# Later 32x32 transposes, longer DMA pieces and later products in the self-attention of the second block

## The chip, the cores and the metric

The kernel runs on one core of a Trainium2 chip. The metric is the device time of one execution in microseconds. TensorE multiplies matrices into PSUM, VectorE (DVE) and ScalarE (ACT) read PSUM and SBUF, GpSimd (POOL) and SyncE (SP) issue most of the DMAs. Each engine runs its own instructions in a fixed order and waits on semaphores for the others.

## The reference

Four attention blocks run in sequence on `x` of 4 batches x 1024 tokens x 256 channels (float32). Their context is 4 x 77 x 256. Block L1 is the one that matters here. It has three layers; the first attends to the context, and the second and third attend to themselves, with 4 heads of 64 channels over 1024 tokens:

```python
Q = relu(q @ Wq + bq); K = relu(k @ Wk + bk); V = relu(v @ Wv + bv)   # 4 heads of 64
scores = einsum('hbqd,hbkd->hbqk', Qh, Kh) / sqrt(64)
scores = where(key_mask == 0, NEG, scores)
attn = softmax(scores, axis=-1) * query_mask
out = einsum('hbqk,hbkd->hbqd', attn, Vh)
out = layer_norm(out + q, gamma, beta)
enc = leaky_relu(out @ Wff + bff, 0.2) + out
```

For the product with V the softmax numerators, which come out with queries on the partitions, must be turned so that keys are on the partitions.

## The kernel before

Work is cut into items: one layer for one batch. The two self layers of L1 are eight items of class `Self4`, and each has 16 units. A unit (`scores(p, t)`) is one pair of heads `p` (two of the four) and one tile `t` of 128 queries against all 1024 keys. Two consecutive units, `t` even and `t` odd, share one tile `PR` and one tile `PT`, and are called a pair below.

What happens to a unit, in order:

1. TensorE forms the scores of both heads (L1262) in two PSUM tiles `ss` of two banks each. The pool `pb` has just these two, so the next unit's scores wait until this unit's exponentials have read them.
2. VectorE takes each head's maximum (L1273, tile `nm`). ScalarE takes the exponential (L1279) and writes it to `PR`, sorted so that blocks of 32 keys which go to the same 32 partitions stand together (index `c`).
3. VectorE turns all 32x32 blocks of the unit in place (`turned_by_blocks`, L1291).
4. After the odd unit, 16 DMAs (L1298) carry 32 partitions x 4 KB each from `PR` to `PT`, one for each pair of a source group `a` and a target group `c` of 32 partitions. SP issues eight and POOL eight. This completes the turn.
5. TensorE multiplies by V (`weighted`, L1334), half of the keys in one unit and the other half in the next, and one unit later `normal` scales the result and adds it to `x`.

`PR` (tag E) and `PT` (tag B) have two buffers each. The exponential of the first unit of a pair can therefore start only when all 16 DMAs of the pair before last have landed.

TensorE's order is written by hand: `Pipe.unit` issues, for each unit, what is due as "full", the scores, what is due as "next", a share of other steps (`pump`: projections and transposes of neighbouring items, the feed-forward of the item before), and then what is due as "turn", "late" and "col". `pipe.later(kind, delay, f)` puts a step `delay` units ahead. The orders of VectorE, ScalarE, SP and POOL are made by a scheduler when the program is built. `tc.issue_after(ins)` binds what is issued inside its block behind `ins` in the order of the engine; it adds no wait. The attribute `net.blocks` is true in the branch that runs here.

Of the kernel before, what the change touches and what calls it, by code (L numbers as in the profile page):

```python
# [13 lines left out]
ALU = mybir.AluOpType  # L14
AX = mybir.AxisListType
PSUM = bass.MemoryType.PSUM

P = 128
NB, S, C, SC = 4, 1024, 256, 77
NT = S // P  # L20
# [102 lines left out]
class Pipe:  # L123
# [15 lines left out]
    def unit(self, scores=None, cost=0.0):  # L139
        self.call("full")  # L140
        if scores:
            scores()
        self.call("next")
        self.now += cost
        self.pump()
        for kind in ("turn", "late", "col"):
            self.call(kind)
        self.u += 1

    def run(self, items):  # L150
        pump = Pump(self, 1, items[0].start(), [])
        pump.until(lambda: items[0].halves >= 1)
        left = pump.lists[0]
        before = None
        for a, b in zip(items, items[1:]):
            b.prev = a
        for i, item in enumerate(items):
            last = i + 1 == len(items)
            first = left + ([] if last else items[i + 1].start())
            second = (before.end() if before else []) + (item.end() if last else [])  # L160
            left = []
            idle = item.idle()
            self.pump = pump = Pump(self, item.units + idle, item.more() + first, second)
            for _ in range(idle):
                self.unit()
            for scores in item.attend():
                self.unit(scores, item.cost)
            assert last or not any(pump.lists)
            before = item
        while self.due:  # L170
            pump.n = 0
            self.unit()
        pump.n = pump.units - 1
        pump()
# [33 lines left out]
class Cross16(Item):  # L208
# [147 lines left out]
    def scores(self, g, c):  # L356

        net, h = self.net, H16
        nc = net.nc
        e, s = g // 2, g % 2  # L360
        if g % 2 == 0:
            self.pts = net.tile("B", [SC, 2, h.J, 512], name="PT")
        pt = self.pts[:, g % 2]
        pbs = [net.pb.tile([P, 2, 512], F32, tag="pb", name="pb") for _ in range(2)]
        for j in range(h.J):
            rows = slice(32 * j, 32 * j + 32)
            nc.tensor.matmul(  # L367
                pbs[j // 2][:SC, j % 2, :], self.ka[rows, e, 2 * (j % 2) + s, :], self.qt[rows, e, ts(c, 512)],
                start=True, stop=False,
            )  # L370
        for j in range(h.J):
            rows = slice(32 * j, 32 * j + 3 * G)
            nc.tensor.matmul(  # L373
                pbs[j // 2][:SC, j % 2, :], net.pick16[rows, g, :], self.sh[rows, c, :], start=False, stop=True
            )
        for i in range(2):
            nc.scalar.activation(pt[:, 2 * i : 2 * i + 2, :], pbs[i][:SC], AF.Exp, scale=self.l.scale)  # L377
        net.pipe.later("col", 0, lambda: self.weighted(g, c, pt))

    def weighted(self, g, c, pt):  # L380
        net, l, h = self.net, self.l, H16
        nc = net.nc
        po = net.p1.tile([P, 512], F32, tag="p1", name="po")
        for j in range(h.J):
            col = self.head(g, j) * h.vs
            nc.tensor.matmul(  # L386
                po[ts(j, h.slot), :], l.v[:, self.b, col : col + h.vw], pt[:, j, :], start=True, stop=True
            )
        ot = net.tile("OT", [P, 512], name="OT")
        net.evac(ot, po)  # L390
        net.pipe.later("late", 1, lambda: self.normal(g, c, ot))
# [249 lines left out]
class Layer16Self:  # L641


    scale, norm, eps, out, ff, has_wo = 0.25, 1, None, None, None, True
# [168 lines left out]
class LayerFew:  # L813
# [3 lines left out]
    scale, norm, eps, out, ff, has_wo = 0.25, 1, None, None, None, True  # L817
# [303 lines left out]
class Self4(Item):  # L1121
# [133 lines left out]
    def scores(self, p, t):  # L1255
        net = self.net
        nc = net.nc
        ss = [net.pb.tile([P, 2, 512], F32, tag="pb", name="ss") for _ in range(2)]
        for k in range(2):
            for h in range(2):  # L1260
                rows = slice(64 * h, 64 * h + 64)
                nc.tensor.matmul(  # L1262
                    ss[h][:, k, :], self.qk[p][rows, 0, ts(t, P)], self.qk[p][rows, 1, ts(k, 512)],
                    start=True, stop=True,
                )
        if not net.blocks:
            pr = net.tile("E", [P, 2, S], name="PR")
        elif t % 2 == 0:
            self.pr = net.tile("E", [P, 2, 2, S], name="PR")
        for h in range(2):  # L1270
            at = slice(2 * p + h, 2 * p + h + 1)
            s2 = ss[h].rearrange("p k n -> p (k n)")
            nc.vector.tensor_reduce(self.nm[:, t, at], s2, AX.X, ALU.max, negate=True)  # L1273
            if net.blocks:
                out = self.pr[:, t % 2, h, :].rearrange("p (c k i) -> p k c i", c=4, i=32)
                s2 = s2.rearrange("p (k c i) -> p k c i", c=4, i=32)
            else:
                out = pr[:, h, :]
            nc.scalar.activation(out, s2, AF.Exp, bias=self.nm[:, t, at], accum_out=self.sums[:, t, at])  # L1279
        if net.blocks:  # L1280
            net.pipe.later("next", 1, lambda pr=self.pr: self.turned_by_blocks(p, t, pr))
        else:
            net.pipe.later("full", 1, lambda: self.turned(p, t, pr))

    def turned_by_blocks(self, p, t, pr):


        net = self.net
        nc = net.nc
        part = pr[:, t % 2].rearrange("p h s -> p (h s)")  # L1290
        nc.vector.transpose(part, part)  # L1291
        if t % 2 == 0:
            return

        pt = net.tile("B", [P, 2, 2, 4, NT, 32], name="PT")
        for c in range(4):
            for a in range(4):
                (nc.sync, nc.gpsimd)[a % 2].dma_start(  # L1298
                    out=pt[ts(c, 32), :, :, a].rearrange("p t h k j -> p (t h) (k j)"),
                    in_=pr[ts(a, 32), :, :, ts(c, 256)].rearrange("p t h n -> p (t h) n"),  # L1300
                )
        state = []
        for half in range(2):
            net.pipe.later("turn", 2 + half, lambda half=half: self.weighted(p, t, pt, half, state))

    def turned(self, p, t, pr):

# [16 lines left out]
    def weighted(self, p, t, pts, half, state):  # L1324
        net = self.net
        nc = net.nc
        if half == 0:
            state.append(net.p1.tile([P, 2, P], F32, tag="p1", name="po"))
        po = state[0]
        if net.blocks:  # L1330
            po = po.rearrange("p t (a j) -> p t a j", a=4)
        for k in range(4 * half, 4 * half + 4):
            for h in range(2):
                nc.tensor.matmul(  # L1334
                    po[64 * h : 64 * h + 64], self.v[:, k, 64 * (2 * p + h) : 64 * (2 * p + h) + 64],
                    pts[:, :, h, :, k, :] if net.blocks else pts[:, :, h, k, :], start=k == 0, stop=k == NT - 1,
                )
        if half:
            if t % 4 == 1:
                self.ot = net.tile("OT", [P, 4, P], name="OT")  # L1340
            at = t % 4 - 1
            net.carry(self.ot[:, at : at + 2, :], state[0])
            if at:
                net.pipe.later("late", 1, lambda ot=self.ot: self.normal(p, t - 3, ot))
# [853 lines left out]
```

## Time and profile before

| | |
|---|---|
| median of 3 runs | 2405.5 us (2398.03 to 2406.79) |
| profiled execution, its own time | 2396.79 us |
| its span, first to last instruction | 2394.9 us |
| granted TensorE clock, mean of the span | 0.958 |
| busy share of the span: TensorE, VectorE, ScalarE, POOL | 92%, 66%, 39%, 16% |
| first and last maximum of the self layers (L1273) start | 950.2 us, 1874.0 us |
| a transpose (L1291), mean of 128 | 2311 ns |
| an exponential (L1279), mean of 256 | 1114 ns |
| a maximum (L1273), mean of 256 | 1210 ns |
| issue of a DMA from PR to PT: POOL, SP, median | 552 ns, 806 ns |

The profiled execution is the base of every duration. Busy time is summed over an engine's instructions; matmuls are pipelined and their ends are modelled, so that a matmul that waits in the middle of a group shows as a longer one. "Idle before" is the time an engine stood still ahead of an instruction, put down to what released it.

### The profile page before, as it was taken

Reading aid. Unit: us, or ns where it says so; the run is one execution under the profiler, and the core shown is the slowest. Engines: PE = TensorE matmul, PEld = TensorE weight load, DVE = VectorE, ACT = ScalarE, POOL = GpSimd, SP = SyncE. Lnnn points to the kernel's source line nnn. Section 1 sums busy time; section 2 is a strip of 40 time slices with the busy share of each in tenths; the row PEclk is TensorE's granted clock in tenths of the full one; section 3 lists DMA queues with packets and bytes.
Section 4 is the critical chain, followed back from the end, with each engine's and each line's share of the span. In section 5 each row is a group of like instructions: output and inputs, shape, how many; then the busy total and the mean of one; then the engine's idle time right before and its main releaser. Section 6 shows DMA issues by size and latency. Waiting matters only on the chain. (4 is left out here: it accounts for less than half of the span.)

```text
span 2394.9 us, 31195 instructions
## 1 busy us (share of the span) xinstructions
PE 2204.3 (92%) x11035; PEld 1204.8 (50%) x11035; DVE 1582.6 (66%) x3167; ACT 930.2 (39%) x1828; POOL 380.4 (16%) x648
## 2 busy tenths in 40 slices
PE   6899999999898979999999899999999899999996
PEld 3565446566577655545454445454545344444442
DVE  6665553534424565888888788888888656656765
ACT  2222332222232355545454454444444234434333
POOL 2000000000000000333333233333333100000000
PEclk8999989989998998999999999999999899999988
DMA  5000010000000000667776577766787400000000
GB/s 147 1 3 14 5 36 1 1 3 5 12 1 7 1 5 1 146 147 152 151 156 144 123 151 157 151 142 141 148 163 143 97 5 1 5 1 1 27 18 28
DMA packets 148677, 158.01 MB, mean 66 GB/s; under 512 B 51432, under 2 KB 130849, under 8 KB 148513
## 3 DMA queue, kind: packets, MB, share of 16 engines
q1 hardware_dynamic: 122161, 85.63, 17.2%
q0 software_dynamic: 25296, 69.24, 13.1%
q8 instruction: 91, 1.49, 0.3%
q10 hardware_dynamic: 1056, 1.05, 0.1%
q14 instruction: 73, 0.60, 0.1%
HBM read 17.41 MB, written 4.19 MB: 9 GB/s over the span
## 5 line engine op out<-in xcount | busy, mean ns | idle before, releaser
L1279 ACT ACTIVATE PR<-ss,nm 128x1024 f32<-128x1024 f32 x256 | 284.7, 1114 | 366.2 <-DVE nm L1273 290.2
L1291 DVE STREAM_TRANSPOSE PR<-PR 128x2048 f32<-128x2048 f32 x128 | 295.8, 2311 | 128.9 <-ACT PR L1279 114.3
L1298 POOL DMA_DIRECT2D PT<-PR x512 | 279.6, 554 | 577.7 <-PE ss L1262 236.7
L1262 PE MATMUL ss<-QK 64*128 64x512 f32 x1024 | 324.8, 628 | 28.8 <-ACT PR L1279 28.5
L1273 DVE TENSOR_REDUCE nm<-ss 128x1 f32<-128x1024 f32 x256 | 299.6, 1210 | 13.8 <-PE ss L1262 13.8
L377 ACT ACTIVATE PT<-pb 77x1024 f32<-77x1024 f32 x192 | 185.4, 1015 | 193.2 <-PE pb L373 193.2
L1334 PE MATMUL po<-PT,V 128*64 128x256 f32 x2048 | 251.1, 387 | 5.1 <-DMA PT<-PR 5.1
L281 DVE TENSOR_REDUCE mx<-pa 128x4 f32<-128x308 f32 x384 | 161.4, 470 | 83.7 <-PE pa L276 82.5
L1262 PEld LDWEIGHTS ss<-QK 64*128 64x128 f32 x1024 | 113.3, 187 | 176.8 <-ACT PR L1279 99.7
L1334 PEld LDWEIGHTS po<-PT,V 128*64 128x64 f32 x2048 | 136.6, 137 | 108.4 <-issue 51.1
L276 PE MATMUL pa<-KA,QT 64*128 64x308 f32 x768 | 169.1, 486 | 14.0 <-DVE mx L281 12.8
L1545 POOL TENSOR_TENSOR pw<-va,minus_half 128x4 f32<-128x4 f32 (+1 forms) x28 | 38.8, 1384 | 714.5 <-DVE va L1543 542.0
L386 PE MATMUL po<-PT,Vc 77*32 77x512 f32 x768 | 140.4, 639 | 7.6 <-ACT PT L377 7.0
L276 PEld LDWEIGHTS pa<-KA,QT 64*128 64x128 f32 x768 | 84.3, 193 | 99.1 <-issue 37.0
L604 PE MATMUL pp<-hF,w 128*128 128x256 f32 x512 | 116.9, 382 | 0.0
L367 PE MATMUL pb<-QT,KA 32*77 32x512 f32 x768 | 114.1, 665 | 0.0
L619 PE MATMUL pp<-w,hid 128*128 128x256 f32 x512 | 113.7, 379 | 0.0
L619 PEld LDWEIGHTS pp<-w,hid 128*128 128x128 f32 x512 | 97.0, 190 | 16.5 <-issue 2.2
L604 PEld LDWEIGHTS pp<-hF,w 128*128 128x128 f32 x512 | 95.6, 190 | 18.2 <-issue 6.0
L266 PE MATMUL pp<-hT,wq 128*128 128x512 f32 x192 | 98.0, 646 | 5.5 <-ACT hT L1507 5.0
L1536 DVE BATCH_NORM_STATS2 st<-x 128x6 f32<-128x256 f32 x256 | 97.7, 403 | 3.2 <-DMA x<-in_x 2.3
L1405 PE MATMUL pp<-wo,hE 128*128 128x256 f32 x384 | 96.4, 393 | 1.6 <-ACT hE L1512 1.6
(256 smaller groups left out, 3079.5 us busy)
## 6 DMA issues: line engine op xcount, KB each, us to landing
PT<-PR SPq DMA_DIRECT2D x512, 128.0 KB
PT<-PR POOLq DMA_DIRECT2D x512, 128.0 KB, 4.9
x<-in_x SPq DMA_DIRECT2D x4, 1024.0 KB
out<-x SPq DMA_DIRECT2D x8, 512.0 KB
w<-in_ff_w SPq DMA_DIRECT2D x2, 1024.0 KB
gb<-in_norms POOLq DMA_DIRECT2D x5, 256.0 KB, 6.6
wk<-in_l_wk SPq DMA_DIRECT2D x10, 128.0 KB
wv<-in_l_wv SPq DMA_DIRECT2D x5, 256.0 KB
```

The costliest lines, as they stand in the source:

```text
L276: nc.tensor.matmul(pas[i], self.qt[rows, e, ts(t, P)], self.ka[rows, e, :, :], start=True, stop=True)
L281: nc.vector.tensor_reduce(out, pas[i].rearrange("p (j s) k -> p j s k", s=2), AX.X, ALU.max, negate=True)
L377: nc.scalar.activation(pt[:, 2 * i : 2 * i + 2, :], pbs[i][:SC], AF.Exp, scale=self.l.scale)
L386: nc.tensor.matmul(po[ts(j, h.slot), :], l.v[:, self.b, col : col + h.vw], pt[:, j, :], start=True, stop=True)
L604: nc.tensor.matmul(pp[:, i, :], self.w1[:, cc, ts(f + i, P)], s["hT"][:, cc, ts(q, 2 * P)], start=cc == 0, stop=cc == NC - 1)
L619: nc.tensor.matmul(pp[:, u, :], s["a"][:, f, ts(u, P)], self.w2[:, f, :], start=f == 0, stop=f == NF - 1)
L1262: nc.tensor.matmul(ss[h][:, k, :], self.qk[p][rows, 0, ts(t, P)], self.qk[p][rows, 1, ts(k, 512)], start=True, stop=True,)
L1273: nc.vector.tensor_reduce(self.nm[:, t, at], s2, AX.X, ALU.max, negate=True)
L1279: nc.scalar.activation(out, s2, AF.Exp, bias=self.nm[:, t, at], accum_out=self.sums[:, t, at])
L1291: nc.vector.transpose(part, part)
L1298: (nc.sync, nc.gpsimd)[a % 2].dma_start(out=pt[ts(c, 32), :, :, a].rearrange("p t h k j -> p (t h) (k j)"), in_=pr[ts(a, 32), :, :, ts(c, ...
L1334: nc.tensor.matmul(po[64 * h : 64 * h + 64], self.v[:, k, 64 * (2 * p + h) : 64 * (2 * p + h) + 64], pts[:, :, h, :, k, :] if net.blocks e ...
```

## The change

It does four things in `scores` and `turned_by_blocks`, for the eight self items only. The maxima are remembered, and the transpose of a unit is bound behind the maxima of the unit that follows it. The dimensions of `PR` and `PT` are reordered, so that each of the 16 DMAs reads and writes one run of 4 KB in each partition instead of four of 1 KB. SP issues twelve of them and POOL four (those with `a == 3`). The two halves of the product with V move from the end of the third and fourth unit after the pair to just behind the scores of the fourth and fifth.

```diff
-            self.pr = net.tile("E", [P, 2, 2, S], name="PR")
+            self.pr = net.tile("E", [P, 4, 2, 2, S // 4], name="PR")
...
-            nc.vector.tensor_reduce(self.nm[:, t, at], s2, AX.X, ALU.max, negate=True)
+            net.reduced = nc.vector.tensor_reduce(self.nm[:, t, at], s2, AX.X, ALU.max, negate=True)
             if net.blocks:
-                out = self.pr[:, t % 2, h, :].rearrange("p (c k i) -> p k c i", c=4, i=32)
+                out = self.pr[:, :, t % 2, h, :].rearrange("p c (k i) -> p k c i", i=32)
...
-        part = pr[:, t % 2].rearrange("p h s -> p (h s)")
-        nc.vector.transpose(part, part)
+        part = pr[:, :, t % 2].rearrange("p c h n -> p c (h n)")
+        with net.tc.issue_after(net.reduced.ins):
+            nc.vector.transpose(part, part)
...
-        pt = net.tile("B", [P, 2, 2, 4, NT, 32], name="PT")
+        pt = net.tile("B", [P, 4, 2, 2, NT, 32], name="PT")
         for c in range(4):
             for a in range(4):
-                (nc.sync, nc.gpsimd)[a % 2].dma_start(
-                    out=pt[ts(c, 32), :, :, a].rearrange("p t h k j -> p (t h) (k j)"),
-                    in_=pr[ts(a, 32), :, :, ts(c, 256)].rearrange("p t h n -> p (t h) n"),
+                (nc.gpsimd if a == 3 else nc.sync).dma_start(
+                    out=pt[ts(c, 32), a].rearrange("p t h k j -> p (t h k j)"),
+                    in_=pr[ts(a, 32), c].rearrange("p t h n -> p (t h n)"),
                 )
...
-            net.pipe.later("turn", 2 + half, lambda half=half: self.weighted(p, t, pt, half, state))
+            net.pipe.later("next", 3 + half, lambda half=half: self.weighted(p, t, pt, half, state))
...
-                    pts[:, :, h, :, k, :] if net.blocks else pts[:, :, h, k, :], start=k == 0, stop=k == NT - 1,
+                    pts[:, :, :, h, k, :].rearrange("p a t j -> p t a j") if net.blocks else pts[:, :, h, k, :], start=k == 0, stop=k == NT - 1,
```

## The prediction

> **What bounds the kernel now.** I read the busy times by stage first. The eight self items fill 950 to 1910 us; 1060 to 1780 us is their undisturbed middle. The columns are the stretch, its length, then busy time and count for TensorE, weight loads, VectorE, ScalarE and POOL, the granted clock, the DMA share and GB/s.
>
> ```profile
> 1060.00:1780.00 720.00, 686.52 (x3348) 338.47 (x3344) 599.61 (x778) 342.27 (x701) 231.28 (x412) 0.99 0.70 147
> ```
>
> TensorE looks full. The groups of the same stretch say otherwise (count, then busy time and mean of one, then idle time before them and what ended it):
>
> ```profile
> L1262 PE MATMUL ss<-QK 64*128 64x512 f32 x788 | 247.6, 627 | 18.0 <-ACT PR L1279 17.9
> L1273 DVE TENSOR_REDUCE nm<-ss 128x1 f32<-128x1024 f32 x198 | 231.9, 1211 | 11.9 <-PE ss L1262 11.9
> L1291 DVE STREAM_TRANSPOSE PR<-PR 128x2048 f32<-128x2048 f32 x99 | 228.8, 2311 | 103.2 <-ACT PR L1279 90.3 <-DMA PT<-PR 12.8
> L1279 ACT ACTIVATE PR<-ss,nm 128x1024 f32<-128x1024 f32 x197 | 219.1, 1114 | 295.1 <-DVE nm L1273 233.6 <-issue 40.8 <-DMA PT<-PR 19.2
> L1334 PE MATMUL po<-PT,V 128*64 128x256 f32 x1584 | 192.8, 385 | 0.0
> ```
>
> 198 maxima are 99 units, so a unit lasts 720/99 = 7.27 us. An undelayed group of eight score matmuls takes 1.99 us (next fence), 197 us for 99 units. The 247.6 us shown hold 51 us of waiting inside the groups, and 18 us stand before them. Without these 69 us TensorE needs 651/99 = 6.6 us per unit. ScalarE waits for VectorE (233.6 us), and VectorE hardly waits for scores (11.9 us): it is 83% busy, and stands 103 us ahead of its transposes. So VectorE sets the pace, with maxima 2.36, a wait for the exponentials, transpose 2.31, and the small work between. The timeline of one unit shows that chain:
>
> ```profile
> 1198.58 2.32 DVE L1273 TENSOR_REDUCE nm<-ss 128x1 f32<-128x1024 f32 x2
> 1201.37 1.13 ACT L1279 ACTIVATE PR<-ss,nm 128x1024 f32<-128x1024 f32 x1
> 1202.62 2.31 DVE L1291 STREAM_TRANSPOSE PR<-PR 128x2048 f32<-128x2048 f32 x1 [1.73 <-ACT PR L1279]
> 1204.00 1.99 PE L1262 MATMUL ss<-QK 64*128 64x512 f32 x8
> 1205.00 1.24 SPq L1298 DMA_DIRECT2D PT<-PR  x2
> 1206.02 1.22 DVE L1273 TENSOR_REDUCE nm<-ss 128x1 f32<-128x1024 f32 x1 [0.33 <-PE ss L1262]
> ```
>
> From maxima to the end of the transpose is 6.35 us, with nothing else done. Last, the DMA view of 1195 to 1235 us, one figure per us:
>
> ```profile
> DMA  9999996000068999999990000068999999999007
> GB/s 205 214 268 227 168 199 108 0 0 0 8 136 213 250 224 211 278 228 200 191 160 17 0 16 0 0 133 214 252 228 180 299 234 194 198 207 208 13 0 160
> ```
>
> The transpose ends at 1204.93; 16 DMAs of 128 KB then keep all engines full until 1216.6. The trace's completion updates give 12.4 us from the end of the odd unit's transpose to the last landing (mean of 47 pairs). I call this L.
>
> **The change, part by part.** *The tie.* The transpose of unit u now follows the maxima of u+1 on VectorE (the built order shows maxima, transpose, small work in every unit). Its exponentials are then done, so the wait (90 of the 103 us, 0.9 us per unit) goes. VectorE then needs 599.6/99 = 6.06 us per unit, under TensorE's 6.6. But the small work (6.06 minus 2.36 and 2.31, 1.4 us on average) is uneven. In two of an item's 16 units the layer norm (six to eight passes L1583 and L1586 of 0.47, less overlap) brings it to about 4.2 us, and the unit before each has 2.4. There the maxima come 2.4 + 4.7 - 6.6 = 0.5 and then 0.5 + 4.7 + 4.2 - 6.6 = 2.8 us late. Scores wait only if maxima are over 1.25 us late: the second exponential ends 3.75 us after the maxima begin (3.92 here, 1198.58 to 1202.50, with a copy of ScalarE's between), the three quarters of the next group that need its PSUM tile take 1.6 more (of 1.99), and 6.6 - 5.35 = 1.25. So 1.55 us are lost twice in 16 units, 0.19 per unit: 6.79 us per unit if nothing else binds.
>
> What is late next is the buffer `PR`. Landing used to count from the transpose right behind the exponential; now it counts from the maxima of the next unit: 2.4 (maxima) + 2.3 (transpose) + 0.1, then L. With exponentials of unit 4 waiting for unit 1's DMAs, the loop of four units is: exponentials 2.45, scores of the next unit 1.6, TensorE's work to the scores after that 6.6, then 4.8 and L: 15.45 + L. Per unit it is (15.45 + L)/4. At L = 12.4 that is 6.96, at 10.95 it equals TensorE's 6.6. Where this loop binds, lateness in the heavy units cannot be caught up either, and I add 0.3 instead of 0.19 (at most 2 x 2.8/16 = 0.35). So the unit is 7.26 at L = 12.4, which is today's 7.27, and 6.79 below about 10.9. The whole forecast hangs on L.
>
> *DMAs.* The sixteen move 2.1 MB as before. In this stretch POOL's packets, already 4096 bytes, take 290 ns in the mean, SP's of 1024 bytes 79 ns each, so 317 for 4 KB: 9% less on the half that was SP's, 0.5 us of the burst. When POOL is done (from 9 us after the first issue) SP's packets take 90 ns and the rate falls from some 225 to 170 GB/s; 4 KB packets of POOL, nearly alone, ran at 82 ns per KB. Of twelve SP issues, undelayed one per 0.65 us, the last starts 7.1 us after the first, and the first landing of a burst comes 2.7 us after its issue: L is not under 9.8. At the top, 1.2 us to the first packet, 3.7 us with POOL's four at 225 GB/s, and 1.26 MB at 170 GB/s are 7.4, plus 0.5 for completion: 12.8. With POOL's rate per KB for SP too, the last part takes 1.26 MB at 200 = 6.3 us, and L is 11.7; POOL's pieces for the other target groups run beside SP's first ones, where 270 GB/s occur, and take off up to 0.6. I take 11.3, nearest to POOL's row.
>
> [...]
>
> *Queues.* SP issues four more per pair, 2.5 us, and behind them stand the mask row (L1179), thirds and weights. These are used a unit or more later: 0, at most 10 us over the stage by the one 6.9 us wait for thirds seen. POOL saves four issues of 0.55; its power (L1385) follows sooner, nothing waits for that now. ScalarE's queue behind a late exponential (copies that free PSUM for TensorE) is in the 0.3.
>
> *Products.* They come one group of scores (2 us) later. Today the first product runs 4.9 us after the last packet in the mean; landing moves to M + 4.8 + 11.3 = 16.1 after the maxima that start it, the product to three units, 21 us: still 4.9. Without the move 2.9 would be left, so it hides nothing that was seen. At the end of the stage `normal` comes a unit later: 3 us, between 0 and 7.
>
> *Forms.* The transpose gets four runs of 512 instead of 2048 in a row, the product reads its operand at other strides, the exponential writes at others. No row shows them; the same element counts exclude a gain. I take 0; at the other end 0.2 us per transpose and 13 ns per product (the spread of the other rows with 256 columns, L1190 at 403 and L1405 at 392 ns) are 26 and 27 us, mostly covered if TensorE and VectorE are not both full.
>
> *Sum.* At L = 11.3: 26.75/4 = 6.69, plus 0.3 is 6.99, 0.28 us less per unit. About 120 units run in this regime: 34 us, less 3 at the end. The profiled execution took 2396.8 (span 2394.9 plus 1.9 outside it) and would take 2366; it lies 8.7 below the median of the runs, so the median becomes 2374.
>
> **Rivals.** *TensorE alone is the bound* (L under 10.9): 6.79, 0.48 x 120 = 58 us, minus 3: 2350. For it: SP's first issues of 0.59 and packets as short as 46 ns when little else runs. Against: all engines are full in the burst. With the small work spread better, 6.6 gives 80 us, 2328; the order speaks against that.
>
> *The pieces change nothing*, L stays near 12.4: the wait for the exponential is exchanged for a wait on `PR`, 7.26 against 7.27, plus 3 us: about 2407. For it: bytes, engines and target partitions are the same.
>
> *The ring is slower than what it replaces.* Its place is the exponential of each even unit, waiting for SP's last DMA. At L = 12.8 the unit is 28.25/4 + 0.3 = 7.36, 0.09 x 120 = 11 us, plus 3: 2420; at 13.3, SP backed up half a us more, 7.49, 26 + 3: 2434. It decides from L = 12.7. For it: SP needed 8.06 us for eight issues, and twelve at that pace end at 12 us, with landing after that. Against: its first three take 0.6 each and the rest wait for full engines, which they share with half as much of POOL's.
>
> **How the numbers follow.** Forecast case (L 10.9 to 12) 0.45, TensorE alone 0.17, nothing changes 0.13, slower ring 0.25. About 0.5% is what a measurement of this kernel can tell from no change: 12 us. Faster is the first two, 0.62. The range goes from 2342, somewhat below the TensorE case, to 2424, which takes in the nearer part of the ring case; about 0.2 is left out. As cases of both signs count, the likeliest one's own range is 2355 to 2393.
>
> **What would show it.** In the groups: transposes should lose their idle time before them (103 us here), maxima should gain some for scores, the scores' mean should fall from 627 towards 589 ns, and the exponential's idle time for DMA, 19.2 us here, should grow. Twelve SP issues should end under 10 us after the transpose and the burst under 11. The prediction is wrong if the transpose takes more than 2.4 us, if the burst stays at 11.7 or grows, if ScalarE stands over 100 us for DMA, or if waits for `ss` stay at 69 us.

## The result, and the profile after

The changed kernel took 2543.15 us (median of 4 runs, 2541.49 to 2545.81), beside 2406.14 us for the kernel before on the same chip. The ratio is 1.0577, with a 95% interval of 1.0551 to 1.0603. That is 137 us slower, where 32 us faster was forecast. The profiled execution has a span of 2539.3 us.

The busy times of 1060 to 1780 us, in the columns known from before:

```profile
1060.00:1780.00 720.00, 625.97 (x2799) 301.02 (x2795) 502.83 (x637) 299.89 (x602) 90.93 (x175) 0.90 0.50 123
```

Every engine is less busy than before. A pair of units, which took 14.58 us, takes 17.51 (mean over units 20 to 112). So something makes all of them wait more. The groups of the same stretch:

```profile
L1262 PE MATMUL ss<-QK 64*128 64x512 f32 x656 | 239.8, 716 | 83.1 <-ACT PR L1279 83.1
L1273 DVE TENSOR_REDUCE nm<-ss 128x1 f32<-128x1024 f32 x165 | 194.7, 1217 | 157.3 <-PE ss L1262 157.0
L1292 DVE STREAM_TRANSPOSE PR<-PR 128x2048 f32<-128x2048 f32 x83 | 190.9, 2301 | 0.0
L1279 ACT ACTIVATE PR<-ss,nm 128x1024 f32<-128x1024 f32 x166 | 184.0, 1113 | 142.9 <-DVE nm L1273 139.9 <-DMA PT<-PR 2.3 <-issue 0.3
...
L1513 ACT COPY OT<-po 128x256 f32<-128x256 f32 x41 | 15.3, 373 | 121.1 <-PE po L1335 110.5 <-DVE third L2061 10.6
```

VectorE waits for scores, TensorE's scores wait for exponentials, and the exponentials themselves wait less than before: their idle time went down, for maxima from 233.6 to 139.9 us and for DMA from 19.2 to 2.3. A circle of waits whose last member waits less means that ScalarE stands still before something else. The last line names it. The copy of `OT` out of PSUM had 0.5 us of idle time in the kernel before:

```profile
L1512 ACT COPY OT<-po 128x256 f32<-128x256 f32 x49 | 18.4, 376 | 0.5
```

Now ScalarE stands 121 us ahead of it, 110.5 of them for TensorE's product with V. Another 126 us it stands ahead of the activations of `QK`, `V` and `low` (57.2, 34.4 and 34.8 us; 10 us in all before). An exponential waits behind such a step without a wait of its own. The timeline of one even unit:

```profile
1238.68 1.99 PE L1262 MATMUL ss<-QK 64*128 64x512 f32 x8
1240.60 1.95 PE L1335 MATMUL po<-PT,V 128*64 128x256 f32 x16
1240.70 2.36 DVE L1273 TENSOR_REDUCE nm<-ss 128x1 f32<-128x1024 f32 x2 [0.19 <-PE ss L1262]
1242.60 0.37 ACT L1513 COPY OT<-po 128x256 f32<-128x256 f32 x1 [2.98 <-PE po L1335]
1243.12 1.99 PE L1190 MATMUL pv<-wv,hT 128*128 128x256 f32 x8
1245.15 0.84 ACT L1194 ACTIVATE V<-pv,f 128x256 f32<-128x256 f32 x2 [2.19 <-PE pv L1190]
1245.88 1.11 ACT L1279 ACTIVATE PR<-ss,nm 128x1024 f32<-128x1024 f32 x1
1247.14 3.08 PE L1262 MATMUL ss<-QK 64*128 64x512 f32 x8 [2.02 <-ACT PR L1279]
```

The first head's maximum is there at about 1241.9, half-way through the pair of maxima, and ScalarE has been idle since 1239.6. Yet its next instruction in order is the copy of `OT`, which needs the sixteen products that TensorE has only begun at 1240.60; after that come two activations of `V`, which need the projections that follow the products. The exponential starts at 1245.88, 4 us after it could have, and TensorE, whose next scores need the PSUM that it frees, stands still for 2.02 us. In the mean, an even unit's exponential starts 3.9 us after its maximum (0.16 before the change); an odd unit's starts 0.03 us after it in both.

TensorE pays once more for such waits. The windows of a neighbouring pair, where it waits again (after the stretch and its length come the five engines, then the granted clock):

```profile
1256.00:1260.00 4.00, 4.00 (x27) 2.21 (x23) 3.97 (x9) 0.37 (x1) 0.00 (x0) 1.00 0.00 0
1260.00:1264.00 4.00, 1.97 (x8) 0.74 (x6) 4.00 (x9) 3.03 (x6) 1.50 (x4) 0.95 0.18 40
1264.00:1268.00 4.00, 4.00 (x9) 1.40 (x10) 2.45 (x8) 0.00 (x0) 1.46 (x2) 0.50 0.93 269
```

TensorE's scores and products at the end of these windows:

```profile
1262.84 4.88 PE L1262 MATMUL ss<-QK 64*128 64x512 f32 x8 [2.03 <-ACT PR L1279]
1267.64 3.30 PE L1335 MATMUL po<-PT,V 128*64 128x256 f32 x16
```

At the end of 4 us in which TensorE works for 1.97 the clock begins to fall (0.95), in the next 4 us it is 0.50, and the next sixteen products take 3.30 us instead of 1.95. Over the stretch of 720 us the clock is 0.90, against 0.99 before. The Trainium skill, "TensorE: Matmul & The Clock Gate", Part 1, puts the drop to half after about 3.4 us of idling; here a stretch of 4 us sufficed in which TensorE was busy for half of it.

The DMAs are not what is waited for. The DMA view of 1195 to 1235 us:

```profile
DMA  9999808800000000479998898300000000699968
GB/s 213 254 316 262 217 21 205 193 0 0 0 0 0 0 0 0 102 217 254 238 328 246 217 217 201 78 8 0 0 0 0 0 0 0 148 299 217 246 242 217
```

The burst is no longer than before, and some eight microseconds of rest lie between two. L is 11.71 us (12.57 before, when all 48 pairs from unit 16 on are taken), and the exponential that reuses `PR` starts 6.33 us after the last landing.

### The profile page after: what moved, and what is told of

It reads as the page before. It is cut to its first block, busy times and chain, and to the rows that moved or that the text cites. A ratio compares the mean times of both kernels' runs of the same rounds, so it can differ in the third digit from the quotient of the medians.

```text
span 2539.3 us, 30866 instructions
## 1 busy us (share of the span) xinstructions
PE 2265.9 (89%) x11035; PEld 1227.4 (48%) x11035; DVE 1587.9 (63%) x3167; ACT 943.8 (37%) x1828; POOL 225.7 (9%) x392
## 3 DMA queue, kind: packets, MB, share of 16 engines
q10 hardware_dynamic: 1056, 1.05, 0.1%
## 5 line engine op out<-in xcount | busy, mean ns | idle before, releaser
L1262 PE MATMUL ss<-QK 64*128 64x512 f32 x1024 | 375.9, 718 | 120.3 <-ACT PR L1279 120.3
L1335 PE MATMUL po<-PT,V 128*64 128x256 f32 x2048 | 281.0, 422 | 1.0 <-DVE mx L281 1.0
L1262 PEld LDWEIGHTS ss<-QK 64*128 64x128 f32 x1024 | 128.9, 211 | 285.6 <-ACT PR L1279 193.6
L1335 PEld LDWEIGHTS po<-PT,V 128*64 128x64 f32 x2048 | 149.2, 150 | 187.8 <-issue 137.3
L1299 POOL DMA_DIRECT2D PT<-PR x256 | 124.9, 494 | 939.1 <-DVE PR L1292 192.9
L276 PE MATMUL pa<-KA,QT 64*128 64x308 f32 x768 | 163.9, 472 | 11.6 <-DVE mx L281 10.0
```

The costliest lines, as they stand in the source:

```text
L276: nc.tensor.matmul(pas[i], self.qt[rows, e, ts(t, P)], self.ka[rows, e, :, :], start=True, stop=True)
L1262: nc.tensor.matmul(ss[h][:, k, :], self.qk[p][rows, 0, ts(t, P)], self.qk[p][rows, 1, ts(k, 512)], start=True, stop=True,)
L1299: (nc.gpsimd if a == 3 else nc.sync).dma_start(out=pt[ts(c, 32), a].rearrange("p t h k j -> p (t h k j)"), in_=pr[ts(a, 32), c].rearrange( ...
L1335: nc.tensor.matmul(po[64 * h : 64 * h + 64], self.v[:, k, 64 * (2 * p + h) : 64 * (2 * p + h) + 64], pts[:, :, :, h, k, :].rearrange("p a ...
```

## Experiments

The first theory: the order of ScalarE, made when the program is built, has copies ahead of the even units' exponentials whose products TensorE forms only after that unit's scores. The rival: the ring of `PR` is slow by itself, and the order only shows what waits for it. The built order can be counted: copies and activations per pair that stand ahead of the even unit's exponentials (after the odd unit's), and those that stand behind them. Delay is the time from an even unit's maximum to its exponential; slack is the time from the last landing to the exponential that reuses `PR`. These, L and the pair are means in the profiled execution of each kernel. Each ratio is to runs of the kernel before on the same chip.

| kernel | ratio to before (95%) | pair, us | ahead / behind | delay | L | slack |
|---|---|---|---|---|---|---|
| before | 1 | 14.58 | 3.44 / 1.85 | 0.16 | 12.57 | 4.38 |
| after | 1.0577 (1.0551 to 1.0603) | 17.51 | 5.25 / 0.42 | 3.89 | 11.71 | 6.33 |
| e1_act_order | 1.0179 (1.012 to 1.0237) | 15.58 | 3.38 / 2.62 | 1.32 | 11.73 | 1.73 |
| e2_split8 | 1.0049 (1.0012 to 1.0086) | 14.75 | 3.60 / 2.06 | 1.79 | 12.11 | 1.06 |
| e3_before_12_4 | 1.0217 (1.0164 to 1.0271) | 15.35 | 4.75 / 0.29 | 1.76 | 12.32 | 6.81 |
| e4_copy_behind | 1.0035 (1.0002 to 1.0067) | 14.71 | 2.94 / 2.73 | 1.74 | 12.13 | 0.96 |
| e5_port_halves | 0.9882 (0.9818 to 0.9946) | 14.23 | 2.94 / 2.73 | 1.22 | 10.84 | 1.27 |
| e6_pieces | 1.001 (0.9975 to 1.0045) | 14.70 | 3.44 / 1.85 | 0.21 | 12.06 | 5.04 |
| e7_tie | 1.0152 (1.0085 to 1.022) | 14.93 | 4.42 / 0.98 | 1.96 | 12.51 | 1.05 |
| e8_bind_some | 1.009 (1.0057 to 1.0124) | 15.26 | 2.77 / 2.90 | 1.33 | 11.70 | 1.45 |
| e9_tie_even | 0.98 (0.976 to 0.9839) | 13.85 | 2.71 / 2.96 | 0.27 | 12.17 | 3.95 |
| e10_no_tie | 0.9913 (0.9889 to 0.9938) | 14.52 | 2.60 / 2.67 | 0.21 | 12.91 | 4.31 |
| e11_products_back | 0.9862 (0.9809 to 0.9915) | 13.97 | 3.54 / 1.52 | 0.14 | 10.77 | 5.24 |
| e12_halves_alone | 1.0008 (0.9985 to 1.0032) | 14.58 | 3.44 / 1.85 | 0.16 | 11.78 | 5.17 |

**e1_act_order.** The changed kernel, with all that a unit issues after its scores bound behind its exponentials:

```diff
+        with self.tc.issue_after(self.exp.ins):
+            self.rest_of_unit(cost)      # due as "next", pump, due as "turn", "late", "col"
```

> The change as it is, and one thing more: in every unit of the self layers, what ScalarE does for the products and projections issued behind the scores (copies and activations that empty PSUM) is bound in ScalarE's order behind that unit's two exponentials. No wait is added or taken away, DMAs, VectorE and TensorE keep their orders. Theory A (the order that the scheduler gave ScalarE: in even units the copies of the same unit's products stand ahead of the exponentials, 3.5 us late per pair): the delay from maximum to exponential in even units falls from 3.5 us under 1.5 us, a pair from 17.5 to about 14.1 us, time 2370 to 2400 us. Theory B (twelve DMAs of SP land late and hold the exponentials through the two PR buffers): the delay stays, 2500 us or more. Theory C (the products stand badly behind the scores on TensorE): 2500 us or more.

It took 2448.27 us: two thirds of the loss come back, and the delay falls from 3.89 to 1.32 us. So the order is a cause. But the time is above the 2370 to 2400 us that were expected. The binding is too broad: it also holds back the copies of `hT` and other steps that nobody had delayed, and TensorE's transposes now wait 23.6 us for `hT` (8.6 before). And the exponentials now wait 91.9 us for landings, where they waited 2.3 in the changed kernel.

**e2_split8.** The changed kernel, with the DMAs dealt eight and eight again:

```diff
-                (nc.gpsimd if a == 3 else nc.sync).dma_start(
+                (nc.sync, nc.gpsimd)[a % 2].dma_start(
```

> The change with the DMAs of a pair issued eight by SP and eight by POOL, as before, in 4 KB pieces. In the built order of ScalarE the even unit's copies then mostly stand behind its exponentials; only the copy of the finished product still stands ahead, in about two of three pairs. Theory A: the product's copy ends 1.2 us after the first maximum, which scores can nearly bear, so 2385 to 2415 us. Theory B: also 2385 to 2415 us, with landing back at 12 us after the transpose. Theory C: unchanged, about 2540 us.

One line brings 2543 down to 2410.06 us, although L is longer than in the changed kernel. Theories A and B both had this range, so the time speaks against C and does not choose between those two. Its groups:

```profile
L1279 ACT ACTIVATE PR<-ss,nm 128x1024 f32<-128x1024 f32 x194 | 215.2, 1111 | 182.9 <-DVE nm L1273 130.5 <-DMA PT<-PR 30.7 <-DMA nrow<-row 7.9
...
L1513 ACT COPY OT<-po 128x256 f32<-128x256 f32 x49 | 18.2, 371 | 94.2 <-PE po L1335 89.0 <-issue 5.2
```

ScalarE's order is nearly that of before, but the copy of `OT` stands ahead of the even unit's exponentials in 32 of 48 pairs. It did so in 47 of 48 pairs before, where its products came ahead of that unit's scores and were done; with the products behind the scores, ScalarE waits for them (the 89 us). The exponentials now do wait for DMA, and the slack is down to 1 us: this is the prediction's ring.

**e3_before_12_4.** The kernel before, with the DMAs dealt twelve and four, and nothing else:

```diff
-                (nc.sync, nc.gpsimd)[a % 2].dma_start(
+                (nc.gpsimd if a == 3 else nc.sync).dma_start(
```

> The kernel before with one part of the change alone: twelve DMAs of a pair from SP and four from POOL, in pieces of 1 KB, transposes and products where they were. The built order of ScalarE changes as it does with the whole change: 4.75 copies stand between an odd unit's and the next even unit's exponentials, instead of 3.44, and 0.29 instead of 1.85 between even and odd. Theory A: most of the loss is here without tie, pieces or moved products; even units' exponentials 2 to 3 us late, 2470 to 2550 us. Theory B: landing later by 1 to 3 us, which the slack of 4 us of the kernel before mostly takes, 2405 to 2440 us. Theory C: 2405 us, no change.

It took 2454.23 us, 2.2% more than before, with transposes, pieces and products as they were. That is between the ranges of the first two theories. The even unit's exponentials wait behind steps of the same kind, here two activations of `V`:

```profile
1219.22 0.37 ACT L1512 COPY OT<-po 128x256 f32<-128x256 f32 x1
1219.49 0.21 ACT L1355 ACTIVATE e<-nm 128x8 f32<-128x8 f32 x1
1223.70 0.84 ACT L1194 ACTIVATE V<-pv,f 128x256 f32<-128x256 f32 x2 [4.00 <-PE pv L1190]
1224.43 1.11 ACT L1279 ACTIVATE PR<-ss,nm 128x1024 f32<-128x1024 f32 x1
```

Over the stretch ScalarE stands 49.2 us ahead of `V` and 69.9 us ahead of `QK` (9.7 and 0.2 before), and no exponential waits for a landing:

```profile
L1279 ACT ACTIVATE PR<-ss,nm 128x1024 f32<-128x1024 f32 x188 | 208.5, 1113 | 197.9 <-DVE nm L1273 197.6
...
L1233 ACT ACTIVATE QK<-pp,qk_bias 128x512 f32<-128x512 f32 x48 | 32.9, 685 | 69.9 <-PE pp L1231 35.3 <-PE pp L1226 34.6
L1194 ACT ACTIVATE V<-pv,f 128x256 f32<-128x256 f32 x48 | 20.1, 472 | 49.2 <-PE pv L1190 49.2
```

In the mean the buffer had been free for 6.8 us. So who issues the DMAs changes the order of an engine that issues none of them. The built order is the same with 1 KB and with 4 KB pieces (before and e6), and it differs with the number of SP's issues. The tie by itself changes it too (e7 in the table). What the issues do to it fits a scheduler which reckons that `PR` comes free late when SP has twelve issues in a row, and fills ScalarE with other work until then; the scheduler's own reckoning was not looked at.

**e4_copy_behind.** e2, with the copy of `OT` alone bound behind the exponentials:

```diff
+            with net.tc.issue_after(net.exp.ins):
                 net.carry(self.ot[:, at : at + 2, :], state[0])
```

> Eight and eight issues as in the run with the split undone, and one binding more: the copy of a finished product (tile OT) stands behind the two exponentials of its unit in ScalarE's order; nothing else is bound. If the copy ahead of the even unit's exponentials is what is left of the loss there, the delay from maximum to exponential in even units falls from 1.8 to under 0.8 us, and time to 2370 to 2395 us. If the two PR buffers hold the exponentials (landing to exponential was 1.1 us in the mean, 0.1 at the tenth percentile), the delay stays at 1.5 us or more, ScalarE's idle time for DMA grows from 31 us, and time is 2395 to 2415 us.

The 94 us ahead of the copy go down to 5.2, and the time stays: 2409.36 us. The exponential's own line says where they went:

```profile
L1279 ACT ACTIVATE PR<-ss,nm 128x1024 f32<-128x1024 f32 x196 | 217.4, 1112 | 254.5 <-DVE nm L1273 138.9 <-DMA PT<-PR 78.6 <-DVE PR L1292 14.3
...
L1514 ACT COPY OT<-po 128x256 f32<-128x256 f32 x49 | 18.1, 369 | 5.2 <-issue 5.2
```

It waits for DMA, 78.6 us instead of 30.7, with 0.96 us of slack in the mean and 0.17 in the lowest tenth. With ScalarE's order mended, the ring of `PR` takes what the tie gave.

**e5_port_halves.** e4, with the sixteen DMAs dealt so that at any time SP carries pieces for target groups 0 and 1 and POOL for 2 and 3:

```diff
-        for c in range(4):
-            for a in range(4):
-                (nc.gpsimd if a == 3 else nc.sync).dma_start(
+        for i in range(8):
+            for spread in range(2):
+                c, a = i // 4 + 2 * spread, (i + 2 * spread) % 4
+                (nc.sync, nc.gpsimd)[spread].dma_start(
```

> The same as the run with the copy bound behind, with the sixteen DMAs dealt out otherwise: SP takes target groups c = 0, 1 and POOL c = 2, 3 at the same time, with the source groups a shifted by two against each other. Bytes, pieces, number of issues per queue and all engine orders are the same. If the burst is limited by which partitions are read and written at one time, landing falls from 12 us after the transpose to 7 to 10 us, the PR buffers no longer bind, a pair takes 13.6 to 14.0 us and time is 2350 to 2375 us. If DMA engines are limited in themselves, landing stays at 11.5 to 12.5 us and time within 6 us of that run.

L falls from 12.13 to 10.84 us, the pair by 0.48, and the time to 2371.85 us, faster than before. The time lies in the range of the first theory, but L is neither in its 7 to 10 us nor in the 11.5 to 12.5 of the other. The windows of 1060 to 1780 us, of e4 and then of e5 (the last two columns are the busy share of the DMA engines and GB/s):

```profile
1060.00:1780.00 720.00, 675.36 (x3304) 334.05 (x3304) 589.15 (x751) 345.62 (x700) 202.97 (x405) 0.97 0.65 146
```

```profile
1060.00:1780.00 720.00, 683.46 (x3404) 340.10 (x3402) 610.67 (x787) 353.51 (x717) 208.12 (x415) 0.98 0.56 151
```

More bytes go in less of the engines' time: the 4 KB packets take 227 ns (POOL) and 238 ns (SP) in the mean, where both took 283 in e4. Both halves of the target partitions are now written at one time; the edit also shifts the source groups against each other, and the two were not told apart. As the kernel's time follows L, the ring does bind in e4.

**e6_pieces.** The kernel before with pieces of 4 KB alone, dealt eight and eight.

> The kernel before with one part of the change alone: pieces of 4 KB, eight issues by SP and eight by POOL, transposes and products where they were; all engine orders equal those of before. Landing falls from 12.6 to about 11.8 us, where the kernel before has 4.4 us to spare: 2395 to 2410 us, no change of more than 0.5%, by every theory.

No difference in time: 2400.31 us. L falls by 0.51 us, which nothing waits for.

**e7_tie.** The kernel before with the tie alone:

```diff
-        nc.vector.transpose(part, part)
+        with net.tc.issue_after(net.reduced.ins):
+            nc.vector.transpose(part, part)
```

> The kernel before with the tie of the transposes alone, pieces of 1 KB, eight and eight. VectorE no longer waits for exponentials before transposes (103 us in 720). The built order of ScalarE has 4.42 copies between odd and next even unit's exponentials (before 3.44) and 0.98 between even and odd (1.85). If the order of ScalarE and the PR buffers (landing 12.6 us after a transpose that comes 5 us later) both bite, a pair takes 14.8 to 15.5 us and time is 2420 to 2470 us. If the tie is a gain by itself, as the prediction had it at this landing time, 14.5 us and 2400 us.

It took 2438.17 us, 1.5% more. The transposes lose their idle time, ScalarE's order changes (4.42 ahead, 0.98 behind), the ring binds (slack 0.18 us in the lowest tenth), and there is a wait for landings of which every other kernel has under 1 us:

```profile
L1335 PE MATMUL po<-PT,V 128*64 128x256 f32 x1533 | 202.7, 410 | 47.8 <-DMA PT<-PR 34.3 <-DMA thirds<-third 5.8 <-DMA nrow<-row 4.5
```

The products with V, which stay where they were, now come up against the landings: 1.38 us behind them in the mean, 0.32 in the lowest tenth.

**e8_bind_some.** The changed kernel (twelve and four) with four kinds of step bound behind the exponentials: the copies of `OT` and the activations of `QK`, `V` and `low`.

> The change as it is (twelve and four issues), with a narrower binding than in the first run: in ScalarE's order only the finished product's copy (OT), the projections' activations (QK, V) and the feed-forward's scaling (low) stand behind the exponentials of the unit that issues them; copies of transposes and the row sums stay free. If the order of ScalarE is the whole loss of the change beyond the PR buffers, this does as well as eight and eight: delay from maximum to exponential in even units 1.2 to 1.8 us, pair 14.5 to 14.9 us, 2395 to 2420 us. If twelve issues by SP cost something on the chip themselves, or the 38 us that the first run stayed above eight and eight were theirs, 2435 us or more.

It took 2422.52 us: 121 of the 137 us come back with SP's twelve issues as they are. What ScalarE waits for is turned round:

```profile
L1281 ACT ACTIVATE PR<-ss,nm 128x1024 f32<-128x1024 f32 x190 | 211.0, 1112 | 308.3 <-DVE nm L1275 191.6 <-DMA PT<-PR 73.5 <-DVE x L1596 13.4
...
L1522 ACT COPY OT<-po 128x256 f32<-128x256 f32 x48 | 17.7, 369 | 2.3 <-PE po L1337 2.3
```

So the order of ScalarE is most of the loss. Yet the run lies between its two expectations: a pair takes 15.26 us, where 14.5 to 14.9 were expected and e2 has 14.75, and TensorE's transposes wait 19.7 us for `hT` (6.0 in e2). By the times e8 is 0.4% slower than e2, with intervals that overlap. Whether the 12/4 dealing costs something beside the order, or the binding does, stays open.

**e9_tie_even.** e5 with the tie for even units alone. The odd unit's transpose, for which the DMAs wait, comes right behind its own exponentials again:

```diff
+        if t % 2:
+            nc.vector.transpose(part, part)
+        else:
+            with net.tc.issue_after(net.reduced.ins):
+                nc.vector.transpose(part, part)
```

> The run with port halves, with the tie for the transposes of even units alone; those of odd units, which start the DMAs, are placed by the scheduler: maxima of the odd unit, transpose of the even one, transpose of the odd one, then the next maxima. DMAs start some 4 us sooner against the exponentials that need the buffers. If the PR buffers are what still holds the port-halves run (1.2 us of delay in even units), the delay falls under 0.4 us and a pair from 14.23 to 13.6 to 13.9 us: 2335 to 2358 us. If two transposes in a row (4.6 us) make VectorE late for the next even unit's maxima, a pair takes 14.2 to 14.6 us: 2370 to 2395 us.

This is the fastest kernel: 2353.33 us, ratio 0.98 (0.976 to 0.9839). The DMAs start a set of maxima and a transpose earlier, the slack grows to 3.95 us, and the delay is 0.27. Its stretch and two groups:

```profile
1060.00:1780.00 720.00, 695.01 (x3512) 349.66 (x3511) 623.16 (x820) 362.99 (x732) 221.17 (x434) 0.99 0.57 156
...
L1273 DVE TENSOR_REDUCE nm<-ss 128x1 f32<-128x1024 f32 x208 | 244.5, 1213 | 61.5 <-PE ss L1262 61.5
...
L1279 ACT ACTIVATE PR<-ss,nm 128x1024 f32<-128x1024 f32 x208 | 231.0, 1112 | 265.1 <-DVE nm L1273 259.2 <-DMA wk<-in_l_wk 4.3 <-ACT xs L1162 1.1
```

No exponential waits for a landing, the clock is back at 0.99, and VectorE now waits for scores: at 6.93 us per unit TensorE, busy for 695 of 720 us, is nearest to being the bound.

**e10_no_tie.** e5 without the tie.

> The run with port halves, without the tie: transposes stand right behind their exponentials again, pieces, port halves, later products and the copy behind the exponentials stay. If the tie is what makes the port-halves run faster than before, VectorE's wait before transposes (103 us in 720 before) comes back and a pair takes 14.4 to 14.6 us: 2385 to 2405 us. If that gain comes from the later products and ScalarE's order, 14.1 to 14.3 us and 2365 to 2378 us.

It took 2386.42 us. The transposes have their idle time again:

```profile
L1291 DVE STREAM_TRANSPOSE PR<-PR 128x2048 f32<-128x2048 f32 x99 | 228.7, 2311 | 92.7 <-ACT PR L1279 76.5 <-DMA PT<-PR 13.7 <-ACT OT L1514 2.5
```

Between e10 and e9 lies the tie of the even units alone, about 1.1% (0.9913 against 0.98, by intervals that do not overlap). The whole tie, in e5, gives 0.3% against e10, which the intervals do not tell from nothing. L is long in e10, 12.91 us, because the first issue comes only 2.5 us after the transpose: SP waits, 80 us of this stretch, for the later products that still read `PT`; with 4.31 us of slack that is not on the path.

**e11_products_back.** e9 with the products with V where they were before the change.

> The kernel of e9 (pieces of 4 KB dealt over both halves of the target partitions, the transposes of even units alone behind the next maxima, the copy of OT behind the exponentials), but with the products with V back behind the other steps of the third and fourth unit after the pair, as before the change. What is open is what the products' move costs by itself. In e9 SP's first issue of a pair stands 1.62 us behind the odd unit's transpose because PT is read until then by the later products. If that wait is on the path, L falls from 12.2 to about 10.8 us and the time goes to 2335 to 2350. If ScalarE's order and TensorE set the pace, as the slack of 3.9 us between the last landing and the exponential in e9 says, the wait costs nothing: the same time within 0.5% (2342 to 2365), with a slack larger by about 1.5 us. Built order of ScalarE: 3.54 copies per pair ahead of the even unit's exponentials and 1.52 behind, nearly as in the kernel before; a delay of the even units' exponentials over 1 us is not expected.

It took 2360.96 us. SP's queue, waits in total, times and longest, first in e9 and then here:

```profile
SPq L1303 <- DVE PR L1292: 188.0, 50, 15.1
SPq L1303 <- PE po L1339: 58.0, 34, 4.5
```

```profile
SPq L1303 <- DVE PR L1292: 233.2, 40, 17.5
...
SPq L1303 <- PE po L1339: 3.1, 1, 3.1
```

In e9 the later products keep `PT` until SP could already issue into it, 1.62 us per pair. Here that wait is gone and L is 10.77 us as expected, but the time is not better: with over 3.9 us of slack in both, landings are not on the path. The intervals of the two ratios overlap: where the products stand makes no difference that these runs can tell.

**e12_halves_alone.** The kernel before with the dealing of e5 alone, in pieces of 1 KB.

> The kernel before with one edit: SP and POOL issue eight DMAs each as before, but at any time the one carries pieces for target groups 0 and 1 and the other for 2 and 3. Pieces stay at 1 KB, transposes right behind their own exponentials, products where they were. If dealing the targets over both halves is what shortened L from 12.1 to 10.8 us in e5, L falls here from 12.6 to about 11.3 us. As nothing waits for landings in the kernel before (4.4 us of slack), the time stays within 0.5% of before. If instead the shorter L of e5 needs pieces of 4 KB, L stays at 12.3 or above.

The time is that of before, 2400.18 us, as L is not on its path. L falls from 12.57 to 11.78 us, 0.8 us where 1.3 were expected: the dealing works with pieces of 1 KB too, and does more with 4 KB.

## Why the prediction was wrong

**The step that failed** is the one on queues: "ScalarE's queue behind a late exponential (copies that free PSUM for TensorE) is in the 0.3." The sentence asks what a late exponential does to copies, and the loss came the other way round, from copies that make an exponential late. Under "The tie" the built order of VectorE was read, and the order of ScalarE was taken to stay as it was. It did not: 5.25 copies and activations per pair stand ahead of the even unit's exponentials instead of 3.44. The price was 3.7 us of delay in each pair, and a clock of 0.90 in its train. The measured pair of 17.51 us is 3.53 above the forecast of 2 x 6.99. e8 shows it from the side of the order, and e3 from the side of the edit: the dealing of twelve and four, which had been costed at "0, at most 10 us" for what stands behind it in SP's queue, costs 2.2% in the kernel before, where no exponential waits for a landing. The whole change costs 5.8%, the tie alone 1.5% (e7), and all but the dealing 0.5% (e2). So the dealing and the other parts together do more than each by itself; no run has the dealing and the tie without the moved products, and their shares stay open. How much of the 3.53 us is delay and how much is the halved clock was not separated either: no run changed the one without the other. An estimate bounds the clock's part. In this trace the granted clock is 1.00 or 0.50 and nothing between, so a mean of 0.90 is a fifth of the time at half, 3.5 us of a pair, and that costs TensorE at most half of it, 1.75 us.

**The second step that failed** is the size of the loop through `PR`. With the order mended and dealt eight and eight, e4 was 0.35% slower than before, where the formula with its L of 12.13 gives (15.45 + 12.13)/4 + 0.3 = 7.20 us per unit; the pair took 14.71, 7.36 per unit. This excess, 0.16 us per unit or 0.6 in the loop of four units, is more than the 0.07 us of gain that the formula leaves at this L (7.27 to 7.20). At e5's 10.84 the formula gives 6.87, and 7.12 were measured. So the slope is about right (0.32 us per unit forecast, 0.24 measured) and the 15.45 is 0.6 to 1.0 us short. With twelve and four (e8) it is over 2 us short. What makes the loop longer than its terms stays open in all three. The rival "the ring is slower than what it replaces" named the right place, the exponential of each even unit, but the wrong cause, SP's last DMA: its point of decision was L over 12.7, and the ring binds in e4 at 12.1.

**What held.** The transposes lose all their idle time (103.2 to 0.0 us), and the reordered dimensions cost nothing (transposes of 2301 ns after 2311, and products of 385 ns in e6 as before). Twelve SP issues end 9.3 us after the transpose, under 10. L is 11.71 us, where 11.3 was taken, from 10.9 to 12; the working had 11.7 before it took off 0.6 for pieces that run side by side. So the term on which "the whole forecast hangs" was nearly right, and it was not on the path. The products' move by itself makes no difference where ScalarE's order is mended (e9 and e11). In the changed kernel it had a side that the text did not see: the copy of `OT` stays ahead of the exponentials while its products go behind the scores, which is the 110 us of the result. And without the move something shows, against the text: in e7, with the tie alone, 1.4 us are left between landing and product, not 2.9, and TensorE waits 34 us there. Of the 1.5 us between the two figures 1.2 are e7's longer L (12.51 against 11.3), as its pieces are still of 1 KB.

**The signs.** Of the signs that were to speak against the forecast, the one that came true is "waits for `ss` stay at 69 us", in a worse form: the scores' mean went from 627 up to 716 ns and the idle time before them from 18 to 83 us. The exponentials' idle time for DMA was to grow and fell to 2.3. Here that wait shrank where growth was expected because ScalarE was held earlier in its own order.

**Pieces and halves.** Pieces alone (e6) took L down by 0.5 us, to 12.06. The Trainium skill, "SBUF — State Buffer", the section on issuing two DMAs to hit both halves, says that two transfers at one time, one to each half of the partitions, gain only 6% over a single one. No run here has one or two transfers alone. With sixteen dealt over both halves the whole of L, issue and completion included, became 6% shorter with 1 KB pieces (e12) and 11% with 4 KB (e5, against e4), and for these sixteen the measurement decides.

## What to carry to other kernels

Where a scheduler makes the order of the engines, an edit to who issues a DMA can reorder an engine that has nothing to do with it: read the built order of every engine that shares a buffer with the edit, not only of the one that is edited. When an engine's waits for the suspected cause go down while everything waits for it, look whether its own order holds it: its other instructions' idle time says by what. And of a pair of steps that fill one buffer, delay only the step that does not end the filling: the tie on even units gave the gain that the tie on both gave back.

## What the runs showed of the hardware

TensorE's granted clock fell to 0.50 behind a stretch of 4 us in which it was busy for 2, and sixteen products then took 3.30 us instead of 1.95: there a wait of some 2 us on another engine was paid twice. Of these sixteen DMAs between SBUF partitions, the length of pieces mattered less than where they go at one time: from 1 KB to 4 KB L fell by 0.5 us, and by dealing the targets over both halves by 0.8 to 1.3 us.
